# Expert pages closed by scatters instead of filled beforehand, inner values of an expert numbered by rows

## The chip, the cores and the metric

The kernel runs on one core of one Trainium2 chip. The metric is the device time of one launch in microseconds (us); lower is better. Engines are named as in the profile: PE is TensorE (PEld is its weight load), DVE is VectorE, ACT is ScalarE, POOL is GpSimd, SP is the engine that issues most of the transfers here.

## The reference, cut to what matters

12,500 nodes with 256 features pass through a graph layer and then through a layer of eight experts, each with a residual:

```python
x = x + gnn(layernorm(x))     # msgs = feat[src] * w; agg = segment_sum(msgs, dst); agg @ W.T + b
x = x + moe(layernorm(x))
# moe: logits = x @ gate_w + gate_b; idx = argmax; prb = softmax(logits)[idx]
#      pos = place of the token among those of its expert; kept = pos < C   (C = 1954)
#      buf[idx, pos] = x
#      hmid = relu(buf @ w1 + b1)           # (E, C, 1024)
#      y = (hmid @ w2 + b2)[idx, pos] * prb * kept
```

There are 212,500 edges, sorted by destination. E = 8, D = 256, F = 1024 inner values for each expert; everything is float32. One expert's w1 is 256 x 1024 (1 MB), its w2 is 1024 x 256 (1 MB). The numbering of the 1024 inner values is free: any permutation used for the columns of w1, for b1 and for the rows of w2 alike gives the same y.

## The kernel before, in words

**Stages.** First `table()` (lines 722 to 804): x is loaded in 13 chunks, normalised and stored to `feat` in DRAM, while the first 70 groups of 128 edges are already gathered from x itself. Then one loop (lines 806 to 839) that interleaves everything else by hand. Last `rest()` (lines 527 to 553).

**The loop.** One turn of the loop issues one gather: `gather(s)` (line 579) is an indirect transfer that POOL issues, 128 rows of 1 KB by source index, into one of 32 buffers `m`. 16 turns later the group is used: DVE builds the weighted one-hot matrix `h` (line 587), PE multiplies (line 596) and accumulates 15 groups to a block `ws` (line 599). `nodes()` forms each tile of 128 nodes from these blocks (lines 632 to 646). Every 8 tiles (a chunk) `route()` computes the gates with `gw_sb` (line 267), the expert and the place of each token. Then POOL writes the tokens, 128 at a time, to `buf` in DRAM by an indirect transfer (`put`, line 329). A row of `buf` has 2056 B: the normalised token, the residual, the gate value and the token's number.

**Pages.** `buf` has 128 pages of 128 rows, 16 for each expert, and two more that are empty. `listing()` lists the pages that have become full; `experts()` (line 658) computes them in the loop, 33 times two pages of one expert at once ("pairs") and 17 times one page ("singles"; the three last chunks list singles). `load()` (line 417) brings a page and, for each load anew, that expert's b1, b2, w1 and w2, all issued by SP in this order (lines 427, 434, 436, 438, 440). `pg` has two buffers, each weight tile three. `products()` (line 455) computes the inner values in 8 steps of 128: for each, 2 matmuls with a 128-column slice of w1 as the stationary operand (line 464), then relu with bias on ACT (line 468), then 8 matmuls with w2 (line 475). `finish()` adds b2, scales, adds the residual (the last reading of `pg` is the cast of the token numbers, line 503), and POOL writes the rows of `out` by token number (`send`, line 506).

**Empty rows.** `fill()` (lines 228 to 235) writes the constant FILL to all 130 pages, 10 pages in a transfer, at the beginning of the loop: 13 transfers on SP. A row that no token came to therefore carries a token number beyond N, and `send` drops it.

**The rest.** After the loop each expert has at most one page that is partly filled. `last()` (lines 400 to 415) finds their numbers `lp`; `rest()` loads two of them ahead and computes the eight as singles. A page that `listing` still lists would follow under `tc.If(left > 0)`; it does not occur with these data.

**Order.** Instructions of an engine run in the order in which the program text emits them (`tc.manual_schedule`), so a wait holds up all that stands behind it on its engine. Semaphores are inserted from the tiles that instructions read and write; `declare_no_dep` removes single dependences by hand.

Of the kernel before, what the change touches and what calls it, by code (L numbers as in the profile page):

```python
# [9 lines left out]
F32 = mybir.dt.float32  # L10
I32 = mybir.dt.int32
U8 = mybir.dt.uint8
AF = mybir.ActivationFunctionType
ALU = mybir.AluOpType
# [4 lines left out]
P = 128  # L19
N = 12500  # L20
D = 256
E = 8
F = 1024
# [7 lines left out]
SKIP = 1 << 20  # L31
# [10 lines left out]
RW = 2 * D + 2  # L42
PE_ = (C + P - 1) // P
NP_ = E * PE_
# [45 lines left out]
def gnn_moe_kernel(ctx: ExitStack, tc: tile.TileContext, x, src, dst, ew, wT, gb, gate_w, gate_b,  # L90
                   w1, b1, w2, b2, out):
    nc = tc.nc

    consts = ctx.enter_context(tc.tile_pool(name="consts", bufs=1))
    dram = ctx.enter_context(tc.tile_pool(name="dram", bufs=1, space=DRAM))

    feat = dram.tile([N, D], F32, name="feat")
    buf = dram.tile([(NP_ + 2) * P, RW], F32, name="buf")

    ident = consts.tile([P, P], F32, name="ident")  # L100
    make_identity(nc, ident)
    ones = consts.tile([P, P], F32, name="ones")
# [4 lines left out]
    pcol = consts.tile([P, 1], F32, name="pcol")  # L107
# [20 lines left out]
    page_of = consts.tile([P, 2], F32, name="page_of")  # L128
# [5 lines left out]
                            op1=ALU.add)  # L134
# [79 lines left out]
    class Ffn:  # L214
# [11 lines left out]
            nc.vector.memset(taken, 0.0)  # L226

        def fill(self):
            fill = self.p3.tile([P, RW], F32, name="fill", bufs=1)
            nc.vector.memset(fill, FILL)  # L230
            v = buf.rearrange("(a p) d -> p a d", p=P)
            for a in range(0, NP_ + 2, 10):
                n = min(10, NP_ + 2 - a)
                nc.sync.dma_start(v[:, a:a + n, :], fill[:, None, :].to_broadcast([P, n, RW]))
                yield

        def psum(self, name):
            return self.ps_m.tile([P, 512], F32, name="ms")
# [161 lines left out]
        def last(self):  # L400
            p3 = self.p3
            c8 = p3.tile([P, E], F32, name="c8")
            nc.vector.tensor_mul(c8, run, mine)
            c = p3.tile([P, 1], F32, name="c1")
            nc.vector.tensor_reduce(c, c8, axis=AX.X, op=ALU.add)
            nc.vector.tensor_scalar(c, c, float(C), page0, op0=ALU.min, op1=ALU.subtract)
            some = p3.tile([P, 1], F32, name="some")
            nc.vector.tensor_scalar(some, c, 1.0, None, op0=ALU.is_ge)
            nc.vector.scalar_tensor_tensor(some, c, float(P), some, op0=ALU.is_lt, op1=ALU.mult)
            nc.vector.tensor_scalar(c8, mine, some, None, op0=ALU.mult)  # L410
            pi = self.psum("pi")
            nc.tensor.matmul(pi[0:1, :E], page_of[:, 0:1], c8, start=True, stop=True)
            lp = p3.tile([1, E], I32, name="lp", bufs=1)
            nc.vector.tensor_scalar(lp, pi[0:1, :E], float(NP_ * P), None, op0=ALU.add)
            return lp

        def load(self, of, li, i, e=None):
            p4 = self.p4
# [12 lines left out]
        def weights(self, e):  # L431
            p4 = self.p4
            b1_sb = p4.tile([P, F // P], F32, name="b1_sb", bufs=3)
            nc.sync.dma_start(b1_sb, b1[:, ds(e, 1), :].rearrange("p a f -> p (a f)"))
            b2_sb = p4.tile([P, D], F32, name="b2_sb", bufs=3)
            nc.sync.dma_start(b2_sb, b2[ds(e, 1), :].rearrange("a d -> (a d)").partition_broadcast(P))
            w1_sb = p4.tile([P, 2, F], F32, name="w1_sb", bufs=3)
            nc.sync.dma_start(w1_sb, w1[ds(e, 1)].rearrange("a (k p) f -> p (a k) f", p=P))
            w2_sb = p4.tile([P, F // P, D], F32, name="w2_sb", bufs=3)
            nc.sync.dma_start(w2_sb, w2[ds(e, 1)].rearrange("a (f p) d -> p (a f) d", p=P))  # L440
            return w1_sb, w2_sb, b1_sb, b2_sb


# [11 lines left out]
        def products(self, of, pg, w1_sb, w2_sb, b1_sb, b2_sb, xT, between=None):  # L455
            p4, n = self.p4, of * P
            hT = p4.tile([P, F // P, 2 * P], F32, name="hT", bufs=1)
            per = 512 // n
            for f0 in range(0, F // P, per):
                ph = self.ps_h.tile([P, 512], F32, name="ph")  # L460
                for f in range(f0, f0 + per):
                    c = (f - f0) * n
                    for k in range(2):
                        nc.tensor.matmul(ph[:, c:c + n], w1_sb[:, k, f * P:(f + 1) * P],  # L464
                                         xT[:, k * n:(k + 1) * n], start=(k == 0), stop=(k == 1))
                for f in range(f0, f0 + per):
                    c = (f - f0) * n
                    nc.scalar.activation(hT[:, f, :n], ph[:, c:c + n], AF.Relu, bias=b1_sb[:, f:f + 1])  # L468
                yield 1
            if between:  # L470
                between()
            py = self.ps_y.tile([P, 2, D], F32, name="py")
            for a in range(of):
                for f in range(F // P):
                    nc.tensor.matmul(py[:, a, :], hT[:, f, a * P:(a + 1) * P], w2_sb[:, f, :],  # L475
                                     start=(f == 0), stop=(f == F // P - 1))
                    if f == 3 or f == 7 and a < of - 1:
                        yield 1
            self.out = self.finish(of, pg, py, b2_sb)
# [45 lines left out]


        def rest(self):
            lp = self.last()
            got, turned = {}, {}
            for e in range(2):  # L530
                got[e] = self.load(1, lp, 0, e)
            through(self.listing(1, LEFT, count=True))
            turned[0] = self.turn(*got[0][:2])
            for e in range(E):
                if e + 2 < E:
                    got[e + 2] = self.load(1, lp, 0, e + 2)

                def between():
                    if e + 1 < E:
                        turned[e + 1] = self.turn(*got[e + 1][:2])  # L540

                through(self.products(*got[e], turned[e], between))
                through(self.out)
            left = nc.values_load(left_i, min_val=0, max_val=LEFT,  # L544
                                  skip_runtime_bounds_check_because="a count of pages")
            with tc.If(left > 0):
                self.sends, self.before = [], None
                for i in range(4):
                    self.page(1, self.li, i)
                with tc.If(left > 4):  # L550
                    self.sends = []
                    for i in range(4, LEFT):
                        self.page(1, self.li, i)


    with tc.tile_pool(name="edges", bufs=1) as edges:
# [8 lines left out]
        with tc.tile_pool(name="p2", bufs=32) as p2, tc.tile_pool(name="p2h", bufs=12) as p2h, \  # L565
                tc.tile_pool(name="p2o", bufs=2) as p2o, tc.tile_pool(name="p3", bufs=2) as p3, \
                tc.tile_pool(name="p4", bufs=2) as p4, tc.tile_pool(
                    name="ps_e", bufs=2, space=PSUM) as ps_e, tc.tile_pool(
# [153 lines left out]
            def table():  # L722
                nc.sync.dma_start(src_i, src.rearrange("p g j -> p (g j)"))
                xts, lns, vs, ss, batch, sq = {}, {}, {}, {}, {}, {}
                n = len(LCH)
# [73 lines left out]
                            product(k)  # L799
                nc.sync.dma_start(wT_sb, wT.rearrange("(k p) o -> p k o", p=P))  # L800
                nc.sync.dma_start(gb_sb, gb.partition_broadcast(P))
                nc.sync.dma_start(gw_sb, gate_w.rearrange("(k p) e -> p k e", p=P))
                nc.sync.dma_start(gateb_sb, gate_b.partition_broadcast(P))
                return (n - 1) * RB
# [169 lines left out]
```

## Time and profile before

| | us |
|---|---|
| median of 17 runs | 3582.01 |
| lowest, highest run | 3562.75, 3590.15 |
| the profiled execution | 3590.23 |
| its span, first to last instruction | 3588.4 |
| time around the span | 1.8 |
| stage `table()` | 0 to 181 |
| the 13 transfers of `fill()`, first to last issue | 196.0 to 289.0 |
| first and last `put` | 378.3, 3405.0 |
| first page load | 620.3 |
| last gather | 3337.4 |
| `last()` begins | 3473.4 |

The mean granted PE clock is 0.761. How to read the profile: a row of a group gives line, engine, operation, output<-input, count, then the busy time, the mean ns of one, and how long the engine had been idle before and what ended that. Rows of the waits give "engine, instruction <- what it waited for: total us, times, longest us". In the timeline a row gives start, duration, engine, line, operation, and how many instructions are merged in it. The windows give, for a stretch, the busy time and count of each engine, the granted clock, the busy share of the DMA engines and GB/s.

### The profile page before, as it was taken

How to read it: one execution, taken by the hardware profiler on the slowest of the kernel's cores; microseconds unless marked ns; L12 is line 12 of the kernel's file. 1: busy time of each engine (PE TensorE's matmuls, PEld its weight loads, DVE VectorE, ACT ScalarE, POOL GpSimd, SP SyncE). 2: the span in 40 equal slices, each digit the busy share in tenths (PEclk: the TensorE clock that was granted, in tenths of full speed). 3: DMA queues.
4: the chain of work that ended last, by engine and by line, in shares of the span. 5: the costliest groups of instructions: out<-in, count | busy, mean ns of one | idle time of the engine just before them, and what ended most of it. 6: DMA issues, size and time to landing. Idle time of an engine off the chain costs nothing. (4 is left out here: it accounts for less than half of the span.)

```text
span 3588.4 us, 31128 instructions
## 1 busy us (share of the span) xinstructions
PE 2046.2 (57%) x9078; PEld 1701.4 (47%) x9078; DVE 1102.1 (31%) x4115; ACT 540.1 (15%) x1418; POOL 1794.0 (50%) x1859
## 2 busy tenths in 40 slices
PE   1364455655656556565474565566557555466865
PEld 1243344544545445454364354455456443355765
DVE  5542223223224224133232332323323322323421
ACT  6910000100101001011011011011011000011322
POOL 4276565545545553653744645555554455554100
PEclk8577677876877778687686687788778677687988
DMA  7597333523533442542542534433343242354665
GB/s 243 178 326 259 90 98 113 170 73 106 172 100 95 147 135 65 165 138 64 169 135 77 157 99 124 145 106 118 118 134 98 87 146 85 109 175 144 190 199 175
DMA packets 267822, 495.51 MB, mean 138 GB/s; under 512 B 45027, under 2 KB 162229, under 8 KB 267640
## 3 DMA queue, kind: packets, MB, share of 16 engines
q0 software_dynamic: 91920, 251.53, 23.0%
q1 hardware_dynamic: 136210, 203.42, 18.1%
q10 hardware_dynamic: 39510, 38.41, 3.3%
q8 instruction: 81, 1.33, 0.2%
q14 instruction: 101, 0.83, 0.1%
HBM read 399.69 MB, written 97.44 MB: 139 GB/s over the span
## 5 line engine op out<-in xcount | busy, mean ns | idle before, releaser
L579 POOL DMA_INDIRECT m<-feat,src_i x1591 | 1520.9, 956 | 703.4 <-issue 379.4
L596 PE MATMUL pw<-m,h 128*128 128x256 f32 x3322 | 1016.7, 436 | 255.8 <-DVE h L587 130.2
L596 PEld LDWEIGHTS pw<-m,h 128*128 128x128 f32 x3322 | 696.5, 222 | 388.5 <-issue 225.0
L587 DVE TENSOR_SCALAR h<-cols,rel,w_sb 128x128 f32<-128x128 f32 x1661 | 500.1, 357 | 688.9 <-remote 305.2
L464 PE MATMUL ph<-gT,w_sb 128*128 128x256 f32 (+1 forms) x1856 | 388.6, 362 | 244.3 <-issue 150.9
L464 PEld LDWEIGHTS ph<-gT,w_sb 128*128 128x128 f32 x1856 | 323.5, 210 | 290.3 <-issue 185.7
L506 POOL DMA_INDIRECT out<-z,tok x91 | 91.7, 1008 | 671.2 <-DVE h L587 438.1
L632 PE MATMUL ms<-s,ws 128*128 128x128 f32 x1116 | 201.7, 320 | 363.3 <-ACT ws L599 212.8
L632 PEld LDWEIGHTS ms<-s,ws 128*128 128x128 f32 x1116 | 193.6, 231 | 387.4 <-ACT ws L599 217.1
L475 PE MATMUL py<-w_sb,hT 128*128 128x256 f32 x1456 | 373.0, 403 | 3.1 <-issue 3.1
L641 PE MATMUL ms<-wT_sb,aT 128*128 128x256 f32 x392 | 132.1, 469 | 392.5 <-ACT aT L636 340.6
L644 DVE TENSOR_TENSOR rt<-xt,ms 128x256 f32<-128x256 f32 x98 | 41.2, 420 | 1005.2 <-PE ms L641 681.3
L475 PEld LDWEIGHTS py<-w_sb,hT 128*128 128x128 f32 x1456 | 295.8, 206 | 47.4 <-issue 2.4
L468 ACT ACTIVATE hT<-ph,b_sb 128x256 f32<-128x256 f32 (+1 forms) x464 | 167.2, 426 | 866.3 <-remote 484.5
L641 PEld LDWEIGHTS ms<-wT_sb,aT 128*128 128x128 f32 x392 | 86.3, 230 | 427.4 <-ACT aT L636 360.3
L329 POOL DMA_INDIRECT buf<-rt,to x98 | 111.8, 1141 | 324.4 <-DVE c L358 236.8
L267 PE MATMUL ms<-gw_sb,xT 128*128 128x8 f32 x392 | 71.7, 292 | 158.2 <-issue 81.7
L267 PEld LDWEIGHTS ms<-gw_sb,xT 128*128 128x128 f32 x392 | 68.0, 242 | 195.6 <-ACT xT L262 107.7
L599 ACT COPY ws<-pw 128x256 f32<-128x256 f32 x111 | 41.1, 370 | 708.8 <-remote 345.1
L485 DVE TENSOR_TENSOR y<-py,b_sb 128x512 f32<-128x512 f32 (+1 forms) x58 | 33.4, 576 | 302.7 <-PE py L475 287.2
L636 ACT COPY aT<-ms 128x256 f32<-128x256 f32 x98 | 36.5, 372 | 568.8 <-remote 372.5
L579 POOL DMA_INDIRECT m<-in_x,src_i x70 | 68.4, 977 | 81.1 <-PE pw L596 61.0
(156 smaller groups left out, 1153.0 us busy)
## 6 DMA issues: line engine op xcount, KB each, us to landing
w_sb<-in_w SPq DMA_DIRECT2D x116, 1024.0 KB
buf<-fill SPq DMA_DIRECT2D x13, 2570.0 KB
m<-feat,src_i POOLq DMA_INDIRECT x1591
pg<-buf SPq DMA_DIRECT2D x33, 514.0 KB
xt<-in_x ACTq DMA_DIRECT2D x97, 128.0 KB
xt<-in_x SPq DMA_DIRECT2D x12, 1024.0 KB
feat<-xn ACTq DMA_DIRECT2D x12, 1024.0 KB
out<-rt ACTq DMA_DIRECT2D x11, 1024.0 KB
```

The lines of the kernel that those rows point to most:

```text
L267: nc.tensor.matmul(pl[:rows, :], xT[:, k, :rows], gw_sb[:, k, :], start=(k == 0), stop=(k == 1))
L329: s = nc.gpsimd.indirect_dma_start(out=buf[:, :], out_offset=bass.IndirectOffsetOnAxis(ap=to[:, j, :], axis=0), in_=rt[:rows, j, :], in_of ...
L464: nc.tensor.matmul(ph[:, c:c + n], w1_sb[:, k, f * P:(f + 1) * P], xT[:, k * n:(k + 1) * n], start=(k == 0), stop=(k == 1))
L468: nc.scalar.activation(hT[:, f, :n], ph[:, c:c + n], AF.Relu, bias=b1_sb[:, f:f + 1])
L475: nc.tensor.matmul(py[:, a, :], hT[:, f, a * P:(a + 1) * P], w2_sb[:, f, :], start=(f == 0), stop=(f == F // P - 1))
L506: s = nc.gpsimd.indirect_dma_start(out=out[:, :], out_offset=bass.IndirectOffsetOnAxis(ap=to[:, a, :], axis=0), in_=z[:, a, :], in_offset= ...
L579: nc.gpsimd.indirect_dma_start(out=m, out_offset=None, in_=x[:, :] if k < RAW else feat[:, :], in_offset=bass.IndirectOffsetOnAxis(ap=src_ ...
L587: nc.vector.tensor_scalar(h, cols, rel[:, k:k + 1], w_sb[:, k:k + 1], op0=ALU.is_equal, op1=ALU.mult)
L596: nc.tensor.matmul(product.pw, hs.pop(k), ms.pop(k), start=(j == 0), stop=last)
L632: nc.tensor.matmul(pa[:, k * P:(k + 1) * P], sums[g][:, k * P:(k + 1) * P], shifts[t, g], start=(g == gs[0]), stop=(g == gs[-1]))
L641: nc.tensor.matmul(px[:rows, :], aT[:, k * P:k * P + rows], wT_sb[:, k, :], start=(k == 0), stop=(k == 1))
L644: nc.vector.tensor_add(x1, xs[t][:rows, :], px[:rows, :])
```

## The change

- `fill()` fills only the two empty pages, by one transfer in place of 13. The filled SBUF tile is kept.
- `last()` computes, beside `lp`, a table `behind`: for each expert, the row numbers of its last page from the first free row on; rows that hold tokens, and experts without such a page, get numbers beyond the bound. `load_last()` is new: before the last page of an expert is loaded, POOL scatters the filled tile to those rows (numbers beyond the bound are dropped). The load of that page waits for this scatter.
- Inner value number 8p + f is now computed in step f, row p (before: 128f + p). So the slice of w1 in line 464 takes every eighth column; w2 is loaded with 8 consecutive rows (8 KB) in each partition in one piece, in place of 8 pieces of 1 KB; and b1 is brought to the new order once, by 8 transfers from DRAM to a DRAM tile `b1_of`, issued by SP at the end of `table()`, from where `weights()` loads it.

```diff
+    b1_of = dram.tile([E, P, F // P], F32, name="b1_of")
...
         def fill(self):
-            fill = self.p3.tile([P, RW], F32, name="fill", bufs=1)
+            fill = self.fill_rows = self.p3.tile([P, RW], F32, name="fill", bufs=1)
             nc.vector.memset(fill, FILL)
             v = buf.rearrange("(a p) d -> p a d", p=P)
-            for a in range(0, NP_ + 2, 10):
-                n = min(10, NP_ + 2 - a)
-                nc.sync.dma_start(v[:, a:a + n, :], fill[:, None, :].to_broadcast([P, n, RW]))
-                yield
+            nc.sync.dma_start(v[:, NP_:, :], fill[:, None, :].to_broadcast([P, 2, RW]))
+            yield
...
             nc.vector.tensor_scalar(c8, mine, some, None, op0=ALU.mult)
+            both = p3.tile([P, 2, E], F32, name="both")
+            nc.vector.tensor_scalar(both[:, 0, :], c8, page_of[:, 0:1], None, op0=ALU.mult)
+            nc.vector.tensor_scalar(both[:, 1, :], c8, c, None, op0=ALU.mult)
             pi = self.psum("pi")
-            nc.tensor.matmul(pi[0:1, :E], page_of[:, 0:1], c8, start=True, stop=True)
+            nc.tensor.matmul(pi[:, :2 * E], ones, both.rearrange("p a e -> p (a e)"), start=True,
+                             stop=True)
             lp = p3.tile([1, E], I32, name="lp", bufs=1)
             nc.vector.tensor_scalar(lp, pi[0:1, :E], float(NP_ * P), None, op0=ALU.add)
-            return lp
+
+            nc.vector.tensor_scalar(both[:, 0, :], pi[:, :E], pcol, float(NP_ * P), op0=ALU.add,
+                                    op1=ALU.add)
+            nc.vector.tensor_scalar(both[:, 1, :], pi[:, E:2 * E], pcol, float(SKIP), op0=ALU.is_gt,
+                                    op1=ALU.mult)
+            behind = p3.tile([P, E], I32, name="behind", bufs=1)
+            nc.vector.tensor_add(behind, both[:, 0, :], both[:, 1, :])
+            return lp, behind
+
+        def load_last(self, lp, behind, e):
+            s = nc.gpsimd.indirect_dma_start(
+                out=buf[:, :], out_offset=bass.IndirectOffsetOnAxis(ap=behind[:, e:e + 1], axis=0),
+                in_=self.fill_rows, in_offset=None, bounds_check=NP_ * P - 1, oob_is_err=False)
+            for i in self.closed:
+                tc.declare_no_dep(s.ins, i.ins, reason="each expert has pages of its own")
+            got = self.load(1, lp, 0, e)
+            for i in self.closed:
+                tc.declare_no_dep(self.loads[-1].ins, i.ins, reason="each expert has pages of its own")
+            self.closed += [s, self.loads[-1]]
+            return got
...
         def weights(self, e):
-            nc.sync.dma_start(b1_sb, b1[:, ds(e, 1), :].rearrange("p a f -> p (a f)"))
+            nc.sync.dma_start(b1_sb, b1_of[ds(e, 1)].rearrange("a p f -> p (a f)"))
...
-            nc.sync.dma_start(w2_sb, w2[ds(e, 1)].rearrange("a (f p) d -> p (a f) d", p=P))
+            nc.sync.dma_start(w2_sb, w2[ds(e, 1)].rearrange("a (p f) d -> p (a f) d", p=P))
...
-                        nc.tensor.matmul(ph[:, c:c + n], w1_sb[:, k, f * P:(f + 1) * P],
+                        nc.tensor.matmul(ph[:, c:c + n], w1_sb[:, k, f:F:F // P],
                                          xT[:, k * n:(k + 1) * n], start=(k == 0), stop=(k == 1))
...
         def rest(self):
-            lp = self.last()
-            got, turned = {}, {}
+            lp, behind = self.last()
+            got, turned, self.closed = {}, {}, []
             for e in range(2):
-                got[e] = self.load(1, lp, 0, e)
+                got[e] = self.load_last(lp, behind, e)
             through(self.listing(1, LEFT, count=True))
             turned[0] = self.turn(*got[0][:2])
             for e in range(E):
                 if e + 2 < E:
-                    got[e + 2] = self.load(1, lp, 0, e + 2)
+                    got[e + 2] = self.load_last(lp, behind, e + 2)
...
                 nc.sync.dma_start(gb_sb, gb.partition_broadcast(P))
+                for e in range(E):
+                    nc.sync.dma_start(b1_of[e].rearrange("p f -> (p f)").rearrange(
+                        "(a q) -> a q", q=P), b1[:, e, :].rearrange("q a -> a q"))
                 nc.sync.dma_start(gw_sb, gate_w.rearrange("(k p) e -> p k e", p=P))
```

## The prediction

> **What bounds the kernel now.** I began with the busy shares and the 40 slices of the page, then the costliest groups, the waits, and last the timelines of three stretches.
>
> ```profile
> PE 2046.2 (57%) x9078; PEld 1701.4 (47%) x9078; DVE 1102.1 (31%) x4115; ACT 540.1 (15%) x1418; POOL 1794.0 (50%) x1859
> ...
> POOL 4276565545545553653744645555554455554100
> ...
> DMA  7597333523533442542542534433343242354665
> ```
>
> No engine is full over the span. The DMA engines are full in one place only, the third slice (179 to 269 us, the only 9; the fourth has 7): that is where the fill runs.
>
> ```profile
> L579 POOL DMA_INDIRECT m<-feat,src_i x1591 | 1520.9, 956 | 703.4 <-issue 379.4
> L506 POOL DMA_INDIRECT out<-z,tok x91 | 91.7, 1008 | 671.2 <-DVE h L587 438.1
> ```
>
> From 181 to 3337 us the spine is POOL's in-order queue: 1591 gathers of 956 ns, nearly every one with 0.3 us of issue before it (1.25 us each), interrupted where the next instruction is a write of results (line 506) or a put and its rows are not ready yet (671 and 324 us idle). Those waits are for the experts' chain PE, ACT, DVE. After 3340 there are no gathers; 10 singles and then the 8 last pages run one after the other, and the chain of one page sets the pace:
>
> ```profile
> 3508.43 0.15 DVE L503 CAST tok<-pg 128x1 int32<-128x1 f32 x1
> 3508.77 0.35 SPq L427 DMA_DIRECT2D pg<-buf  x1
> ...
> 3518.01 3.81 PE L464 MATMUL ph<-gT,w_sb 128*128 128x128 f32 x32 [2.25 <-DMA w_sb<-in_w]
> ...
> 3518.87 0.14 DVE L503 CAST tok<-pg 128x1 int32<-128x1 f32 x1
> ...
> 3529.79 0.15 DVE L503 CAST tok<-pg 128x1 int32<-128x1 f32 x1
> ```
>
> A page ends every 10.4 to 10.9 us. With two page buffers, a load starts when the page two before has been read (3508.43, load at 3508.77), its w1 has landed 9.2 us later (3518.01), and 11.8 us of products and finishing follow: 21.4 us for two pages. PE is busy 67.55 of the 98 us from 3476 to 3574, so it isn't full there.
>
> **The fill goes.** It removes 12 of 13 transfers, 126 of 130 pages, about 33 MB. Does anything wait for it? The windows of the gathers alone, with the fill and a stretch as long without it (columns: stretch, its length, POOL busy and count, granted clock, DMA share, GB/s):
>
> ```profile
> 196.00:306.00 110.00, 76.95 (x76) 0.73 1.04 378
> 420.00:530.00 110.00, 70.16 (x75) 0.67 0.33 93
> ```
>
> 76 gathers against 75: POOL doesn't lose anything to the fill, and PE uses 142 instructions of line 596 there against 120. The first put is at 378 us, after 23.5 us of waiting for the route, long after the fill's last issue at 289. SP's next work is the page load at 620. So this part gives 0. From the other side, one wait is put down to the fill (ACT at line 599, 24.2 us, once); ACT copies a PSUM tile there, which no fill touches, so I read it as a coincidence in time, but keep -24 as an end.
>
> **Closing the last pages.** Before, `lp` starts at 3475.01 and the first load is issued at 3475.98. Added ahead of `lp`: two small DVE operations (about 0.25 each, as lines 406 and 410 with 0.21 and 0.31) and a matmul with 128 columns of weights (0.59 for the pair, line 373, against 0.20): +0.9. Behind `lp`: two more and an addition, +0.7. Then the scatter. A put that waits for the put before it starts 2.81 us after it (3388.08, 3390.89), so issue to landing is 2.8. The load now goes out at 3475.16 + 0.9 + 0.7 + 2.8 + 0.1 = 3479.7 instead of 3476.0: **+3.7**. Behind it on SP stand b1, b2, w1 and w2 of that page, all later by as much, and PE waits for w1 there (6.2 us at 3485.67). The second scatter starts 1.27 later and lands before SP reaches the second load (2.9 after the first). Scatter n (2 to 7, 1.27 us each on POOL) follows the send of page n-3 and has landed some 4 us after that page's cast; load n waits for the cast of page n-2, 10 us later, which hides it (+4 each if not, 24 in all). What POOL has behind them are sends, with 92 us of idle time in this stage.
>
> **b1 in a new order.** Eight transfers of 1024 elements of 4 B on SP after line 801, ahead of the gate weights. No row shows such a transfer. The smallest packets on SP's queue (32 B) take 9 ns in the trace's packet records, those of 1 KB 46 ns: 8192 packets over 8 to 16 DMA engines are 5 to 47 us; issuing costs 8 x 0.35 (line 434) to 8 x 11.2 us (the fill's longest, with a full queue) = 3 to 90. It starts at 149.5. Hidden by: SP has nothing until 196, the gate weights are first used at 353.4, POOL stands still until 181 for the last store of `feat` (issued 178.6). If packets are slow, that store shares the engines: 0 to +10. I take 0, by the 32 B row. [...]
>
> **w2 in one piece.** Per load 1024 packets of 1 KB become 128 of 8 KB. By the packet records 1 KB takes 46 ns and 4 KB 159: 2.9 us on 16 engines become 2.5. 58 loads: -23 us if all of it were waited for. But PE's waits for weights are for w1 (line 464, 31.6 us in 10 times), which goes ahead of w2; before line 475 PE is idle for 3.1 us in all. I take 0 and keep -23; above, longer packets ahead of a gather: PE waits 60 us for gathers altogether, so at most +10.
>
> **Every eighth column of w1.** Line 464 loads 1856 stationary halves (2 for each float32 product), now with a step of 32 B. No row shows a strided weight load. The nearest is a strided moving operand, line 691 (111 columns, 60 B apart), beside a contiguous one of 128 columns at the same low clock:
>
> ```profile
> 16.69 0.76 PE L691 MATMUL ms<-dst_f,ones 1*128 1x111 f32 x2 [16.69 <-DVE xn L209]
> ```
> ```profile
> 1060.62 0.80 PE L632 MATMUL ms<-s,ws 128*128 128x128 f32 x2 [22.10 <-ACT ws L599]
> ```
>
> At this clock 256 columns take 634 ns and 128 take 421, so 17 columns fewer are 28 ns: 0.77 expected contiguous, 0.76 seen. A step of 60 B costs nothing at 1.7 ns per column. But weights at full clock come faster: 32 loads in 3.65 us (singles, 3506.80), 0.89 ns per column; 213 ns per load in pairs (8 in 1.70), where PE is held by the 256 columns of the product. So: nothing by the nearest row; at most doubling if 1.7 ns is a floor for strided columns. Below nothing there is no reason. I take 0.
>
> [...]
>
> **Sum.** Fill 0, closing +3.7, b1 0, w2 0, columns 0: **+3.7**. Against its own execution: 3590.2 + 3.7 = 3593.9. That execution lies 8.2 above the median 3582.0, so the forecast for a median is **3585.7**, "no change": 0.2%, 7.2 us, is what a measurement of this kernel can tell.
>
> **Rivals.**
>
> *Strided weight loads take twice as long (slower).* Place: singles, where weights and products take turns at 114 ns. Each would pay 32 x 114 = 3.65 us; pairs nothing until a load passes 213 ns, which is the point from which it decides everything. In the 18 singles after 3340 two pages are in flight, so half shows: 18 x 1.8 = 33; of the 7 earlier ones, beside gathers, some 5. +38: **3624**. Ends: 0 and 25 x 3.65 = 91. For it: 0.89 ns per column is twice the pace that line 691 tests. Against: line 691.
>
> *They take four times as long.* 456 ns also outrun pairs: 33 x 32 x 243 ns = 257 us, singles 18 x 10.9 = 196; with part hidden, about **3850**.
>
> *The fill or the w2 packets did hold something (faster).* -24 for ACT's wait, up to -23 for w2; half of that sum: **3562**. For it: the full DMA between 200 and 300. Against: 76 gathers to 75.
>
> *The change doesn't do what it says*: if 8 KB rows are cut into small packets again, w2 stays at 2.9 us; time as forecast.
>
> **Chances.** Forecast case 0.50 (its own range 3574 to 3596: +10 for b1 or the packets, -12 for half of w2; of it 0.20 within 0.2%, 0.17 slower, 0.13 faster), doubled loads 0.28, four times 0.07, faster 0.15. So faster 0.28, same 0.20, slower 0.52. The range 3560 to 3640 leaves out the four times (0.07), the doubled loads where they cost over 54 us (0.06) and the larger half of the gains' span (0.05): 0.18.
>
> **What would show it.** Right: the timeline of a last page still has 32 weight loads in about 3.65 us at full clock, and pairs 8 in 1.70; the gathers between 196 and 306 still number about 76; the first load of the last pages comes some 6.3 us after the first operation of `last()` instead of 2.6; the first gather from `feat` stays at 181; packets of 8 KB in about 310 ns. Wrong: a longer row at line 464; a first put earlier than 378 by more than 10 us; the gate weights late for 353 us.

## The result

| | median, us | ratio to before (95%) |
|---|---|---|
| before (47 runs) | 3580.68 | |
| changed (8 runs) | 3669.89 | 1.0252 (1.0234 to 1.0270) |

Slower by 2.5%, 89 us; forecast were 3585.7 and a range up to 3640. The profiled execution of the changed kernel has a span of 3670.1 us, 81.7 more than that of before, at a mean granted clock of 0.767 (0.761).

The kernel before, unchanged, took 2669 and 2667 us in the first two sets and 3603 and 3609 us in the last two, for a reason that no run here shows, so that each experiment is compared only with the runs of before in its own set.

**The profile after.** The page first: the busy row of the tensor engine, the row of the DMA slices, and the group of the gathers.

```profile
PE 2174.4 (59%) x9078; PEld 1853.9 (51%) x9078; DVE 1101.4 (30%) x4120; ACT 540.3 (15%) x1418; POOL 1801.5 (49%) x1867
...
DMA  7653332532542542542542432433433332444554
...
L602 POOL DMA_INDIRECT m<-feat,src_i x1591 | 1518.9, 955 | 733.6 <-issue 383.1
```

The third slice of the DMA row no longer has a 9: the fill is gone. PE and PEld have gained 128 and 153 us of busy time with the same number of instructions, and POOL is idle before its gathers for 30 us more.

Where the time goes is read by setting the same instruction of both traces side by side:

| instruction | before | after | difference |
|---|---|---|---|
| first gather from `feat` | 181.2 | 223.0 | +41.7 |
| first `put` | 378.3 | 415.9 | +37.6 |
| gather 800 | 1550.4 | 1592.6 | +42.3 |
| last gather | 3337.4 | 3382.5 | +45.1 |
| token cast of the 18th page from the end | 3360.4 | 3413.3 | +52.8 |
| `last()` begins | 3473.4 | 3539.8 | +66.4 |
| first load of a last page | 3476.0 | 3545.8 | +69.8 |
| token cast of the last page | 3573.3 | 3653.9 | +80.6 |

Two steps, then: 42 us are lost before the loop has begun and stay lost, and some 36 more between the last gathers and the end. In the 3200 us between, the difference swings between 34 and 49 us, and nothing is gained or lost that persists.

**The first step.** Before, the next store of `feat` after the one at 147.9 goes out at 159.7, and the first gather from `feat` follows at 181.2:

```profile
159.70 0.37 ACTq L165 DMA_DIRECT2D feat<-xn  x1
...
181.24 0.94 POOL L579 DMA_INDIRECT m<-feat,src_i  x1 [29.94 <-PE pw L596]
```

The timeline of SP's queue at the end of `table()`, then that of ACT with its stores of `feat`, then POOL's, all of the changed kernel:

```profile
149.48 56.70 SPq L826 DMA_DIRECT2D b_of<-in_b  x8
206.23 8.41 SPq L828 DMA_DIRECT2D gw_sb<-in_gate_w  x1
```
```profile
147.78 0.39 ACTq L167 DMA_DIRECT2D feat<-xn  x1
181.79 0.37 ACTq L167 DMA_DIRECT2D feat<-xn  x1
182.21 2.56 ACT L794 ACTIVATE m<-m,nb,rs 128x256 f32<-128x256 f32 x5 [22.64 <-DMA b_of<-in_b]
...
200.69 0.58 ACTq L167 DMA_DIRECT2D feat<-xn  x1
```
```profile
150.20 0.95 POOL L602 DMA_INDIRECT m<-in_x,src_i  x1 [0.30 <-PE pw L619]
222.95 2.51 POOL L602 DMA_INDIRECT m<-feat,src_i  x1 [71.80 <-DMA feat<-xn]
```

The eight transfers of `b1_of` keep SP's queue issuing for 57 us. The store of `feat` that follows the one at 147.8 goes out at 181.8; before, it went out at 159.7. The last one goes out at 200.7 instead of 178.6, and POOL, whose first gather from `feat` needs all of `feat`, stands for 71.8 us.

These 41.7 us have two parts. The first is a wait of ACT, which stands for some 22 us before the store of 181.8, although its own work is done at 159.6. The profile puts the wait down to `b_of`, and the semaphores in the trace say how: this store signals on the same semaphore (number 101) as the third transfer of `b_of`, which was issued at 155.2, and ACT may go on when that transfer's last signal comes, at 181.7. No data connects the two; before, nothing was under way on this semaphore at that time. So the last store goes out 22.1 us later. The second part, 19.6 us, lies behind it: from the issue of the last store to the first gather pass 22.3 us instead of 2.6. What the first part costs by itself no run shows, since SP's 4 B packets run until 222.9 us, just when the gather starts.

The DMA view of the stretch from 150 to 220 us, in 40 slices of 1.75 us, shows what the engines did meanwhile (below it packets, MB and share of the 16 engines' time for SP's queue, q1, and ACT's, q10):

```profile
DMA  9999089615935860455859999999975767334943
GB/s 313 270 280 22 0 10 0 1 0 6 1 0 1 1 1 0 1 1 36 40 37 48 35 53 69 71 48 98 74 49 22 34 9 2 2 1 8 3 21 26
...
q1 hardware_dynamic: 8730, 0.43, 39.6%
q10 hardware_dynamic: 2128, 2.11, 34.0%
```

From 157 to 181 us they are marked busy for about half of the time and move 10 GB/s or less; from there to 206 us they are at 0.5 to 0.9 with 22 to 98 GB/s, where the first slices show 270 and more, and then at 0.3 to 0.9 with 26 GB/s or less. SP's queue takes 39.6% of the engines' time to move 0.43 MB. In the packet records from 149 to 225 us its 8318 packets of 4 B have a median of 9 ns but a mean of 51, and the 1 KB packets of the stores beside them a mean of 168 ns (51 before, from 149 to 185).

**The second step.** The group of the weight loads of the first product (columns: shortest, median, longest in ns, first and last start), before and changed, and two of the last pages in the timeline:

```profile
L464 PEld LDWEIGHTS ph<-gT,w_sb x1856: 186/190/339, 667.6 to 3566.4; 128*128 128x128 f32 x186
```
```profile
L487 PEld LDWEIGHTS ph<-gT,w_sb x1856: 312/337/342, 713.9 to 3646.8; 128*128 128x128 f32 x186
```
```profile
3565.85 7.72 PEld L487 LDWEIGHTS ph<-gT,w_sb 128*128 128x128 f32 x32
3566.07 7.70 PE L487 MATMUL ph<-gT,w_sb 128*128 128x128 f32 x32
3569.34 0.15 DVE L526 CAST tok<-pg 128x1 int32<-128x1 f32 x1
3578.73 7.72 PEld L487 LDWEIGHTS ph<-gT,w_sb 128*128 128x128 f32 x32 [1.69 <-ACT y L511]
...
3580.55 0.14 DVE L526 CAST tok<-pg 128x1 int32<-128x1 f32 x1
```

The shortest record was 186 ns and the median 190; now none is under 312. The 32 loads of a single take 7.7 us instead of 3.65, 240 ns each instead of 114, and the eight last pages end 11.2 to 13.3 us apart (12.1 in the mean) instead of 10.1 to 12.5 (10.7).

**The closing scatters.** From the first operation of `last()` to the first load, timeline of the changed kernel:

```profile
3539.84 0.16 DVE L403 TENSOR_TENSOR c<-run,mine 128x8 f32<-128x8 f32 x1
...
3541.62 0.61 PE L415 MATMUL ms<-both,ones 128*128 128x16 f32 x2 [4.94 <-DVE both L413]
...
3543.17 0.97 POOL L429 DMA_INDIRECT buf<-fill,behind  x1 [1.99 <-DVE c L358]
...
3545.82 0.28 SPq L450 DMA_DIRECT2D pg<-buf  x1
```

5.98 us instead of 2.6: the first load is 3.4 later, where 3.7 was forecast.

### The profile page after: what moved, and what is told of

Same layout as the page of the kernel before. It is cut to its first block, busy times and chain, and to the rows that moved or that the text cites. A ratio compares the mean times of both kernels' runs of the same rounds, so it can differ in the third digit from the quotient of the medians.

```text
span 3670.1 us, 31144 instructions
## 1 busy us (share of the span) xinstructions
PE 2174.4 (59%) x9078; PEld 1853.9 (51%) x9078; DVE 1101.4 (30%) x4120; ACT 540.3 (15%) x1418; POOL 1801.5 (49%) x1867
## 5 line engine op out<-in xcount | busy, mean ns | idle before, releaser
L619 PE MATMUL pw<-m,h 128*128 128x256 f32 x3322 | 1026.0, 439 | 274.3 <-DVE h L610 147.8
L619 PEld LDWEIGHTS pw<-m,h 128*128 128x128 f32 x3322 | 705.9, 225 | 400.8 <-issue 230.6
L487 PE MATMUL ph<-gT,w_sb 128*128 128x256 f32 (+1 forms) x1856 | 492.8, 420 | 231.3 <-issue 122.1
L487 PEld LDWEIGHTS ph<-gT,w_sb 128*128 128x128 f32 x1856 | 464.5, 334 | 253.9 <-issue 133.0
L664 PE MATMUL ms<-wT_sb,aT 128*128 128x256 f32 x392 | 140.9, 495 | 449.1 <-ACT aT L659 377.3
L498 PE MATMUL py<-w_sb,hT 128*128 128x256 f32 x1456 | 380.8, 410 | 2.0 <-issue 1.8
L498 PEld LDWEIGHTS py<-w_sb,hT 128*128 128x128 f32 x1456 | 303.7, 212 | 48.9 <-issue 0.2
```

The costliest lines, as they stand in the source:

```text
L487: nc.tensor.matmul(ph[:, c:c + n], w1_sb[:, k, f:F:F // P], xT[:, k * n:(k + 1) * n], start=(k == 0), stop=(k == 1))
L619: nc.tensor.matmul(product.pw, hs.pop(k), ms.pop(k), start=(j == 0), stop=last)
L664: nc.tensor.matmul(px[:rows, :], aT[:, k * P:k * P + rows], wT_sb[:, k, :], start=(k == 0), stop=(k == 1))
```

## The experiments

The theory with which they began: two separate costs, the `b1_of` transfers before the loop (42 us) and the strided weight loads at the end (33 to 38), with 4 us for the scatters, and nothing for the fill and for w2. Rivals: the early loss comes from the missing fill or from the order of SP's queue; the late loss comes from last pages that wait for their scatters.

### Taking the change apart (first set, before 2669 us)

**e1_b1_host**, the changed kernel without the transfers:

```diff
-                for e in range(E):
-                    nc.sync.dma_start(b1_of[e].rearrange("p f -> (p f)").rearrange(
-                        "(a q) -> a q", q=P), b1[:, e, :].rearrange("q a -> a q"))
...
-        "b1": np.asarray(L0_ffn_b1).reshape(E, F // P, P).transpose(2, 0, 1),
+        "b1": np.asarray(L0_ffn_b1).reshape(E, P, F // P).transpose(1, 0, 2),
```

> The changed kernel without the eight transfers to b1_of: b1 comes from the host already in the new order and is loaded as in the kernel before. Theory: the transfers' 8192 packets of 4 B hold up the last stores of feat, and with them the first gather (222.95 us instead of 181.24). Without them the first gather returns to 181 (within 2 us), the first put to about 378, and the time falls by 38 to 45 us, from 3670 to about 3628. Rival: the early loss comes from the missing fill or the order of SP's queue; then the first gather stays near 223 and the time at 3670.

Measured: 1.0179 (1.0166 to 1.0192). The absolute numbers of the expectation belong to the 3580 us of the first profile and can't be met in this set; the step it is about can: the first gather from `feat` comes at 175.4 us. What is left, 48 us, is the late loss, with that of the scatters in it.

**e2_b1_only**, the kernel before with those three lines added and nothing else.

> The kernel before with one thing added: the eight transfers to b1_of at the end of table(), which nothing reads afterwards. Theory: +42 us by themselves, 3581 to about 3622, with the first gather from feat at about 223 and the first put at 416. Rival (the transfers are only late in company of the rest of the change): within 5 us of 3581.

Measured: 1.0134 (1.0120 to 1.0149), +36 us. First gather at 208.9 us, first put at 362.6 against 331.4 in e1: 33.5 and 31 later. So these three lines alone cause the early loss. ACT's wait is here too: some 19 us for `b_of`, until its store goes out at 172.5.

**e3_fill_only**, the kernel before with the small fill, `behind` and `load_last`, and nothing of the new numbering.

> The kernel before with only the first part of the change: two pages filled instead of 130, the last pages closed by scatters; w1, b1 and w2 numbered and loaded as before. Theory: the fill gives 0 and the scatters cost 3 to 5 us, so about 3585 (within 0.2% of before); the first load of a last page comes 6.0 us after the first operation of last() and the last pages then end 10.4 to 10.9 us apart as before. Rival: the late loss (some 37 us after 3340) comes from the loads of the last pages waiting for the scatters; then +15 to +37 us here, the pages about 12 us apart. Rival: the fill's absence costs the 42 us at the beginning; then +42.

Measured: 1.0024 (1.0013 to 1.0034), +6.4 us. The first gather stays at 175.3, the first load of a last page comes 5.95 us after the first operation of `last()`. Both rivals are out: without the fill nothing is lost at the beginning, and the scatters aren't the late loss.

**e4_cols_w2**, the kernel before with the new numbering (b1 from the host) and nothing else:

```diff
-            nc.sync.dma_start(w2_sb, w2[ds(e, 1)].rearrange("a (f p) d -> p (a f) d", p=P))
+            nc.sync.dma_start(w2_sb, w2[ds(e, 1)].rearrange("a (p f) d -> p (a f) d", p=P))
...
-                        nc.tensor.matmul(ph[:, c:c + n], w1_sb[:, k, f * P:(f + 1) * P],
+                        nc.tensor.matmul(ph[:, c:c + n], w1_sb[:, k, f:F:F // P],
```

> The kernel before with only the new numbering: every eighth column of w1 as weights, w2 in one piece of 8 KB per row, b1 in the new order from the host, no transfers to b1_of; fill and last pages as before. Theory: weight loads of a single take 240 instead of 114 ns, 32 of them 7.7 us instead of 3.65, and the time rises by 30 to 42 us, to about 3617, all of it after 3300 us. Rival (the late loss belongs to the scatters): within 10 us of 3581.

Measured: 1.0167 (1.0154 to 1.0180), +45 us, a little over the range named. The 32 products of a single in its timeline, and below them those of the kernel before in the second set:

```profile
2601.12 7.67 PE L464 MATMUL ph<-gT,w_sb 128*128 128x128 f32 x32
2614.62 7.85 PE L464 MATMUL ph<-gT,w_sb 128*128 128x128 f32 x32 [2.16 <-DMA w_sb<-in_w]
```
```profile
2581.76 3.81 PE L464 MATMUL ph<-gT,w_sb 128*128 128x128 f32 x32 [2.70 <-DMA w_sb<-in_w]
2592.33 3.81 PE L464 MATMUL ph<-gT,w_sb 128*128 128x128 f32 x32 [2.94 <-DMA w_sb<-in_w]
```

Until gather 1500 the two are within 2.6 us of each other. The difference is 4.4 us at the last gather, 17 at the cast of the 18th page from the end, 30 when `last()` begins. (The first trace and that of r1 are one execution each, so a few us of this are theirs.) In pairs the loads also outgrow their cover, but by little: products start every 240 ns instead of 216. 33 pairs of 32 are 25 us of PE, and the loop, which POOL paces, hides them.

### The whole, and the parts without their price (second set, before 2667 us)

**r1_before**, the kernel before again, for its trace.

> The kernel before, unchanged, for its trace on the chip of the experiments, where its runs take 2669 us instead of 3582. Theory: the loop there runs at the pace of POOL's gathers and lacks the standstills of all engines that the first trace shows; the stretch after the last gather is as long as on the first chip (about 250 us from the first of the 18 last singles to the end). No rival; a baseline for the tail of the others.

One time, 2660.4 us. From the cast of the 18th page from the end (2434.3) to the end of the span (2658.5) are 224 us, near the 228 of the first trace; the 250 expected, counted from the beginning of that page some 10 us earlier, were too many. The tail is the same, the difference to 3580 lies in the loop.

**r2_after**, the changed kernel again.

> The changed kernel, unchanged, on the chip of the experiments. Theory: the costs add up: 34.8 (transfers alone) + 43.5 (columns alone) + 6.8 (scatters alone) = 85 us, a ratio of 1.032 of the 2669 us there. Rival: the parts hide each other (the later start is caught up in the loop, or the tail is waiting anyway); then under 65 us.

Measured: 1.0298 (1.0277 to 1.0318), +79.5 us. The parts measured singly make 36 + 45 + 6 = 87; up to 13 us of them may hide each other. The rival, under 65, is out. The first gather is at 210.9.

**e6_all_host**, the changed kernel with w1's columns also permuted by the host, so that each slice is contiguous, and without the transfers:

```diff
-                        nc.tensor.matmul(ph[:, c:c + n], w1_sb[:, k, f:F:F // P],
+                        nc.tensor.matmul(ph[:, c:c + n], w1_sb[:, k, f * P:(f + 1) * P],
...
-        "w1": L0_ffn_w1,
+        "w1": np.asarray(L0_ffn_w1).reshape(E, D, P, F // P).transpose(0, 1, 3, 2).reshape(E, D, F),
```

> The changed kernel with w1's columns and b1 brought to the new order by the host, so that each weight slice is 128 contiguous columns again and no transfer reorders b1; two pages filled, scatters, w2 in one piece as in the change. Theory: weight loads return to 114 ns in singles and the first gather to the time of before, so only the scatters are left: +3 to +7 us against before (0.1 to 0.3%), less what the larger packets of w2 give. Rival (w2 in one piece or the missing fill cost something of their own): +15 us or more.

Measured: 1.0033 (1.0021 to 1.0046), +8.8 us. The transfers and the columns are the two large costs: without them what remains is as much as in e3, and the rival of 15 us or more is out. It is more than 3.4, and the tail shows where some of it may lie: the eight last pages, first to last cast, take 78.2 to 78.9 us in the three traces with scatters and contiguous or nearly contiguous weights (e3, e6, e10) and 70.6 to 77.4 in eight such traces without scatters. In e3 two of the six later loads wait 1.2 to 1.3 us after the cast, in e6 two wait 1.5 to 2.3, where before it is always 0.34. That makes 2 to 3 us; the remainder isn't assigned.

**e7_step2**, the kernel before with slices of every second column:

```diff
-                        nc.tensor.matmul(ph[:, c:c + n], w1_sb[:, k, f * P:(f + 1) * P],
+                        nc.tensor.matmul(ph[:, c:c + n], w1_sb[:, k, f // 2 * 2 * P + f % 2:f // 2 * 2 * P + 2 * P:2]
```

> The kernel before with each weight slice of line 464 taking every second column (a step of 8 B instead of 4): two slices share a block of 256 columns. The inner values are then paired with other b1 entries and rows of w2, so y isn't the reference's; the work is the same. Theory A (any step but one is slow): weight loads of a single take 240 ns, +35 to +45 us. Theory B (the cost grows with the bytes between columns and sets in above some step, up to 16 B at no cost): 114 ns, within 5 us of before. Between them, loads of about 150 to 200 ns would show a cost in proportion to the step.

Measured: 1.0004 (0.9992 to 1.0016). The record of a weight load is 196 ns instead of 190. A step of 8 B costs nothing that can be measured: theory B.

### Sizes and places (third set, before 3603 us)

**e5_w2_only**, the kernel before with w2 in one piece, w1 and b1 permuted by the host.

> The kernel before with the new numbering alone, brought about by the host for w1's columns and b1, and w2 in one piece of 8 KB per row; weight slices contiguous, fill kept, no scatters. Theory: the w2 packets hide nothing that anybody waits for, so within 0.2% (5 us) of before. Rival (they did hold something): 5 to 20 us faster.

Measured: 0.9999 (0.9983 to 1.0014). The packets of 8 KB give nothing that can be measured (-6 to +5 us).

**e8_step4**, slices of every fourth column (`f // 4 * 4 * P + f % 4:f // 4 * 4 * P + 4 * P:4`).

> The kernel before with each weight slice of line 464 taking every fourth column (a step of 16 B); inner values are paired with other b1 entries and rows of w2, so y isn't the reference's, the work is the same. At 8 B a load took 196 ns (190 contiguous), at 32 B 337. Theory A (each column that lies in another 16 bytes than the one before costs a step of its own): 16 B is as slow as 32 B, 240 ns per load in singles, +40 to +45 us. Theory B (the cost grows with the distance): between, 205 to 260 ns of the record, +5 to +25 us. Theory C (it sets in above 16 B): within 5 us of before.

Measured: 1.0101 (1.0075 to 1.0126), +36 us, and 233 ns from one product of a single to the next. 16 B are nearly as slow as 32 B: theory A.

**e9_b1_late**, the changed kernel with the transfers moved behind the fill:

```diff
             nc.sync.dma_start(v[:, NP_:, :], fill[:, None, :].to_broadcast([P, 2, RW]))
             yield
+            for e in range(E):
+                nc.sync.dma_start(b1_of[e].rearrange("p f -> (p f)").rearrange(
+                    "(a q) -> a q", q=P), b1[:, e, :].rearrange("q a -> a q"))
+                yield
```

> The changed kernel with its eight b1_of transfers issued after the transfer of the fill, one in each turn of the loop, when no store of feat is in flight any more. Theory: what costs is that the first gather must wait for stores that share the DMA engines with the 4 B packets. Now it comes at 175 us as in the kernel before; the packets then slow some 50 of the gathers, which 16 turns of lead hide in part: 0 to 20 us of the 33 to 36 are left, so 2712 to 2732 us beside 2746 for the changed kernel. Rival (the 8192 packets take DMA time that is missing wherever they run): 30 us or more left.

Measured: 1.0263 (1.0239 to 1.0287): as slow as the changed kernel (1.0252 in its own runs). My theory falls here, and the rival holds. The first gather is back, at 183.3, and yet the first put comes at 422.7, 45 us later than in e5. The window of 196 to 306 us, the same that the prediction used for the fill (POOL busy and count, clock, DMA share, GB/s at the end), and POOL's timeline within it:

```profile
196.00:306.00 110.00, 48.11 (x45) 0.67 0.86 66
```
```profile
247.62 0.95 POOL L606 DMA_INDIRECT m<-feat,src_i  x1 [5.09 <-PE pw L623]
...
260.50 0.95 POOL L606 DMA_INDIRECT m<-feat,src_i  x1 [9.42 <-DMA m<-feat,src_i]
```

45 gathers where before had 76 (and e5, in this set, 74), with the DMA engines at 0.86 and 66 GB/s. 29 to 31 gathers of 1.25 us are 36 to 39 us; POOL stands for 45.8 us in this window until gathers issued earlier have landed. Now it is the gathers' own packets that are slow: those of 4 KB take 773 ns in the mean between 198 and 310 us, where e5 has 173. So it costs as much without any late store: 8192 small packets pass through engines which somebody needs. Full engines alone don't do this: in e5 the fill keeps them at 1.02 in this window, with packets of 2056 B.

**e10_fill_and_close**, the kernel before with the scatters, the whole fill kept.

> The kernel before with the closing scatters added and the whole fill kept. Theory: the scatters cost 3.4 us at the first last page (its load 5.95 instead of 2.59 us after the first operation of last()), nothing behind it, and the missing fill costs and gives nothing: 3 to 7 us over before, as with the fill taken out (6.8). Rival (leaving the fill out costs some 4 us in the loop): 3 us or less over before; rival (it gave something): 10 us or more over before.

Measured: 1.0010 (0.9990 to 1.0031), +3.6 us (-3.6 to +11). It agrees with the theory, but its interval doesn't separate it from the rivals.

### What it is in the small packets (fourth set, before 3609 us)

**x1_half**: the loop over the transfers runs over `range(0, E, 2)`, added to the kernel before.

> The kernel before with only four of the eight transfers to b1_of at the end of table(), 4096 packets of 4 B, which nothing reads. All eight alone moved the first gather by 33.9 us and the time by 34.8 on a chip where before takes 2669 us. Theory (each small packet costs its share of the DMA engines): half, 15 to 22 us, the first gather as much later. Rival (a fixed cost of holding up the last stores, or of a full queue of SP): 30 us or more, or none.

Measured: 1.0050 (1.0034 to 1.0066), +18 us; the first gather at 200.2, where traces with nothing changed in `table()` have 179.9 to 187.3 (the first, e5, e8, e10, x4). Half the packets, half the cost; it isn't a fixed one. ACT has no wait for `b_of` here: its next store signals on another semaphore and goes out at 158.9, the last one at 177.8. The whole loss lies behind the last store, 22.4 us from its issue to the gather: this part of the price needs no shared semaphore.

**x2_rows**: the same bytes in the order in which they lie.

```diff
+                for e in range(E):
+                    nc.sync.dma_start(b1_of[e], b1[:, e, :])
```

> The kernel before with eight transfers of the same 32 KB to b1_of, but copied in the order in which they lie: 128 rows of 32 B each instead of 1024 elements of 4 B. Theory (the number of packets costs): 1024 packets instead of 8192, so an eighth of the cost, 0 to 6 us. Rival (the cost is that of a transfer or of a copy from DRAM to DRAM): 20 us or more.

Measured: 0.9996 (0.9981 to 1.0012). Eight transfers, 32 KB, from DRAM to DRAM: no cost. SP issues them in 6.6 us.

**x3_other_side**: the same elements to the same places, in the order of the source.

```diff
+                for e in range(E):
+                    nc.sync.dma_start(b1_of[e].rearrange("p f -> (p f)").rearrange(
+                        "(a q) -> q a", q=P), b1[:, e, :])
```

> The kernel before with the eight transfers written the other way round: the same elements go to the same places of b1_of, but in the order of the source, so that 8 elements in a row are read and each is written 512 B from the one before. Theory: still 8192 packets of 4 B, the same cost as with the strided source (+35 us or 1.3% where before takes 2669, +42 where it takes 3582). Rival (the strided reading or the order of writing sets the price): less than half or more than 1.5 times of it.

Measured: 1.0013 (0.9995 to 1.0030), under half the price of e2, whose whole interval lies above: the rival is right. There are still 8320 more packets of 4 B than before, but the first gather comes at 195.5 instead of 223.0 (179.9 to 187.3 without transfers). SP's queue, ACT's wait and the first gather in its timeline:

```profile
151.93 22.19 SPq L805 DMA_DIRECT2D b_of<-in_b  x8
174.16 3.40 SPq L807 DMA_DIRECT2D gw_sb<-in_gate_w  x1
```
```profile
173.93 0.37 ACTq L167 DMA_DIRECT2D feat<-xn  x1
174.34 2.56 ACT L773 ACTIVATE m<-m,nb,rs 128x256 f32<-128x256 f32 x5 [12.29 <-DMA b_of<-in_b]
```
```profile
195.46 0.95 POOL L581 DMA_INDIRECT m<-feat,src_i  x1 [41.75 <-PE pw L598]
```

The issue takes 22 us, where the changed kernel needed 57. What is left of the shift is ACT's wait of some 12 us for the third transfer, on the shared semaphore; behind the last store, issued at 192.8, pass 2.6 us to the gather, as before. So at least two thirds of the price (at most 11 us are left of 32 or more) belong to the order of the elements: each read 256 B from the one before and written next to it, instead of 8 in a row read and each written 512 B from the one before. Whether it is the strided reading or the writing of neighbours by different packets that costs, the runs don't tell.

**x4_step3**, slices of every third column (`f // 3 * 128 + f % 3:f // 3 * 128 + f % 3 + 3 * P - 2:3`).

> The kernel before with each weight slice of line 464 taking every third column (a step of 12 B); slices overlap and are paired with other b1 entries and rows of w2, so y isn't the reference's, the work is the same. Records so far: 190 ns contiguous, 196 at 8 B, 329 at 16 B, 337 at 32 B. Theory A (a step in the price for each column that lies in another 16 bytes, three in four here): about 3/4 of the way, 260 to 310 ns. Theory B (two columns are fetched together where they lie within 16 bytes of the start of the first, whatever the line): about 200 ns, no change in the time. In the time: A +20 to +35 us, B within 0.2%.

Measured: 1.0041 (1.0025 to 1.0057), +15 us. The groups of weight loads of e7 (8 B), x4 (12 B) and e8 (16 B):

```profile
L464 PEld LDWEIGHTS ph<-gT,w_sb x1856: 193/196/338, 546.3 to 2644.1; 128*128 128x128 f32 x186
```
```profile
L464 PEld LDWEIGHTS ph<-gT,w_sb x1856: 250/252/338, 679.7 to 3597.9; 128*128 128x128 f32 x186
```
```profile
L464 PEld LDWEIGHTS ph<-gT,w_sb x1856: 307/329/338, 674.4 to 3605.7; 128*128 128x128 f32 x186
```

| step between columns | record, ns | product to product in a single, ns | ratio to before |
|---|---|---|---|
| 4 B (before) | 190 | 112 | |
| 8 B (e7) | 196 | 118 | 1.0004, +1 us |
| 12 B (x4) | 252 | 175 | 1.0041, +15 us |
| 16 B (e8) | 329 | 233 | 1.0101, +36 us |
| 32 B (e4) | 337 | 238 | 1.0167, +45 us |

Theory A for 12 B asked for 260 to 310 ns and +20 to +35 us, B for 200 and no change; 252 lies between, near A. The records are 6 ns longer than the contiguous one at 8 B, 62 at 12 B, 139 at 16 B and 147 at 32 B. These five steps were measured and no others, and why 12 B lies between isn't shown.

No version here beats the kernel before: of all the parts of the change, the best that any gives is e5's 0.9999.

## Why the prediction was wrong, step by step

- **The fill (0).** Right. In the window view 78 gathers pass in the 110 us from 240 to 350 of the changed kernel, in a stretch without the fill; 76 passed beside it. e3 shows no gain from leaving it out, and e10, which keeps it, differs from e3 by less than the intervals.
- **Closing (+3.7).** Right in its place: 3.4 at the first load. As a whole e3 measures 6.4 (3.5 to 9.1). The sentence "load n waits for the cast of page n-2, 10 us later, which hides it" was not quite so: some loads do wait up to 2 us longer.
- **b1 (0, ends 0 and +10).** Wrong: +42 in the first trace, +36 (32 to 40) alone. The step says "8192 packets over 8 to 16 DMA engines are 5 to 47 us" and "Hidden by: ... POOL stands still until 181 for the last store". Both halves failed. "I take 0, by the 32 B row" took the duration of one packet's record for its price: the packets of 4 B have the same median of 9 ns, but a mean of 51, and the stores' packets beside them grow from 51 to 168 ns. With 42 us for 8192, a packet costs the launch 5.1 ns, and if it is spread over 16 engines, which the trace doesn't show, an estimate is 82 ns of one engine. The slower end of the step's own range, 47 us, was the nearer one. And the cover was the victim: what hid the transfers was a wait for stores whose own packets they slowed. A second wait, ACT's 22 us for a transfer whose semaphore its store shares, is in no term of the prediction. e9 shows that a later place, at the loop's beginning, is no better. The line "if packets are slow, that store shares the engines: 0 to +10" had the slowed store and a quarter of the size. The count of 8192 was right: from 149 to 225 us SP's queue has 8318 records of 4 B, before 116.
- **w2 (0).** Right, by e5. Its packets of 8 KB take 309 ns, where about 310 were forecast.
- **Columns (0; "at most doubling if 1.7 ns is a floor for strided columns").** Wrong choice between two ends that were both on the page. 240 ns for 128 columns are 1.88 ns each: at a step of 32 B there is such a floor. Line 691 reads a moving operand, not a stationary one, at a pace where its weight loads took 283 and 333 ns (288 and 333 at line 632, at a granted clock of 0.50) and a contiguous column already 1.7 ns: a floor of 1.88 would have added only some 20 ns to each of its two halves (an estimate), and of a stationary operand it can say nothing. The row that bore on it was the single's 0.89 ns per column. The prediction named it as the rival's point and still let the slower row decide.
- **The first rival (+38, place: singles).** Right: e4 measures 45 (41 to 48), and pairs hide theirs. Its two shares were 33 for the 18 last singles and 5 for the earlier ones; in e4 against r1, 17 us have already gone by the first cast of those 18 and 29 follow, so the earlier ones cost 12 more than I gave them and the last ones 4 less. That the total came near is partly luck.

Together: 42 for the transfers, about 40 for the columns, 3 to 6 for the scatters, 0 for the rest. The chance of 0.28 for doubled loads already led to 3624; the other 42 us, in no rival, put the time beyond the range.

## What to carry to other kernels

A cover counts only if what is waited for isn't slowed by the transfer that it hides: the fill, with packets of 2056 B, kept the engines full (1.04) and cost the gathers nothing that shows (76 in 110 us beside it, 75 and 78 without), while 4 B packets cost 42 us with a thousandth of its bytes. Look also for a semaphore that two transfers of different queues share: here the later one went out only when the earlier one had landed, some 22 us after ACT's work was done. Price a transfer of single elements by the mean of its own packets (51 ns, at a median of 9) and by what it does to its neighbours' (168 ns instead of 51), or give the data its order on the host (e1) or in runs of 32 B, as in x2. And before a stationary operand is taken with a step, look at the pace of its loads at full clock: in the singles here, where they take turns with products as short as they are, the 112 ns from product to product became 175 at a step of 12 B, 233 at 16 and 238 at 32.

## What the runs showed of the hardware that was not expected

- A weight load of 128 float32 columns takes 190 ns in the record at 4 B from column to column (before), 196 at 8 (e7), 252 at 12 (x4), 329 at 16 (e8) and 337 at 32 (e4).
- 8192 packets of 4 B from DRAM to DRAM, each with a record of mostly 9 ns (51 in the mean, in the changed kernel), cost 32 to 45 us in the two places tried, beside stores (e2) and beside gathers (e9); beside the gathers the DMA engines are marked busy at 0.86 while 66 GB/s pass. The same elements in the order of the source cost 11 us at most (x3), and rows of 32 B nothing that can be measured (x2, 0.9996).
- A store on ACT's queue waited some 22 us (the changed kernel; 19 in e2, 12 in x3) for a transfer on SP's queue that signals on the same semaphore, and not at all in x1, where the store signals on another.
